# Layer 1 of a fused eight-stage kernel: attention and the mixture-of-experts routing written as one ordered loop

## The chip, the cores and the metric

The kernel runs on one core of a Trainium2 chip. The metric is device time in microseconds (us) of one execution. The comparison is against the kernel before, timed in the same way. A core has a matrix engine (PE in the profile, with its weight loads PEld), a vector engine (DVE), a scalar engine for activation functions (ACT), a general engine (POOL) that here also issues the indirect DMAs, and an engine that only issues DMAs (SP). Each engine works through its own queue of instructions in order; engines wait for each other by semaphores.

## The reference

The program is four layers, each an attention-like stage and a feed-forward stage, over 8192 tokens of width 128. The change touches layer 1 alone:

```python
# attention of layer 1 (T = 256 tokens in a sequence, 32 sequences)
xn = layer_norm(x, g, b)
q, k, v = split(xn @ qkv_w + qkv_b)
k = k * sigmoid(xn @ gate_w + gate_b)
q = elu(q) + 1.0
k = elu(k) + 1.0
attn = (q @ k.T) * tril
out = (attn @ v) / (sum(q * cumsum(k)) + 1e-6)
x = x + out

# feed-forward of layer 1: 8 experts of hidden width 512, two for each token, and one shared expert
xf = layer_norm(x)
logits = xf @ gate_w + gate_b
top_w, top_i = top_k(logits, 2)
gw = softmax(top_w)
for e in range(8):
    out += combine[:, e:e+1] * (gelu(xf @ w1[e] + b1[e]) @ w2[e] + b2[e])
x = x + out + gelu(xf @ ws1 + bs1) @ ws2 + bs2
```

Here elu(z) + 1 is max(z, 0) + exp(min(z, 0)).

## The kernel before

The 8192 tokens are 64 tiles of 128 tokens; four tiles make a block of 512 tokens (two sequences), so there are 16 blocks. The residual stream `K.x` stays in on-chip memory for the whole kernel. Instructions are ordered by a scheduler that works from priorities, except inside `manual_schedule`, where the engines named keep the order in which the program writes their instructions. POOL and SP are not named in the regions spoken of here, so their order is the scheduler's.

`l1_attn` (L1244 to L1336) has two halves. The first normalizes all tiles (`normed`, L134, on DVE), turns them on PE (`transpose4`, L141), scales them on ACT into `xnT` (L215), and then for each block computes the gated key `kg` (PE L1274 and L1275, ACT sigmoid L1277, DVE L1278). The second half, for each block, makes the query `qp` (PE L1288), the two elu functions (POOL minimum L1293, DVE minimum L1294, ACT exponentials L1295 and L1296, ACT relu L1297, DVE L1298, POOL addition L1299), the value `vp` with its bias as a one-row float32 matmul (PE L1301, L1305, ACT copy L1309), the products `at` (PE L1313, L1316), the mask (DVE L1321), the output `o` (PE L1325), and the division and residual (DVE L1330 to L1334). This half is not in an ordered region.

`l1_ffn` (L1340 to L1452) follows. It loads the weights of all nine experts, takes the statistics of all 64 tiles (L241 and the short chain in `Norm.steps`), normalizes and turns all tiles into `row` and `xnT`, and computes logits for all tokens with 8-column matmuls (PE L1389). Routing is then one chain on DVE for all 64 tiles: `beaten` ranks the eight logits, `picks` marks the two chosen experts, and `Slots.places` counts tokens per expert (two matmuls and a scan) and gives each token a slot in a DRAM table `rows` that is grouped by expert. `Slots.finish` works out which group of 256 slots belongs to which expert. Then each tile's rows are written to their slots by an indirect DMA, issued by POOL, twice for each tile since two experts are chosen:

```python
for n in range(2):
    S.belongs(row, 0, NT, n)
    nc.gpsimd.tensor_copy(row[:, :, D + 1], weight[:, n, :])
    for j in range(NT):
        S.send(slots[n][:, j : j + 1], row[:, j, :])
```

That is 128 calls of `send` (L473). `belongs` (L368) writes, on POOL, where the result of each row will go back. Beside the sends, the shared expert runs for 16 blocks (PE L1431 for the hidden layer, ACT gelu L1435, PE L1437 and L1443 for the output, DVE L1449 for the residual). Last, `Slots.experts` reads the table in 72 groups of 256 rows (SP fetch, PE, ACT, DVE) and scatters each group's result by two more indirect DMAs (POOL L479). It reads what any tile may have written, so its first fetch waits for the last send. Layer 2 starts after it.

Of the kernel before, what the change touches and what calls it, by code (L numbers as in the profile page):

```python
# [10 lines left out]
F32 = mybir.dt.float32  # L11
# [8 lines left out]
P = 128  # L20
# [1223 lines left out]
def l1_attn(K):  # L1244
    nc, ins = K.nc, K.ins
    with ExitStack() as es:
        sp = K.pool(es, "a1", 1)
        wk = K.pool(es, "a1w", 3)
        w = K.load(sp, "a1_w")
        wq, wkk, wv, wg = (w[:, i * D : (i + 1) * D] for i in range(4))  # L1250
        bv = K.load(sp, "a1_bv")
        cols = K.load(sp, "a1_cols")
        bq, bk, bg, gamma, beta = (cols[:, i : i + 1] for i in range(5))
        mean, r2 = K.norm_of_x.mean, K.norm_of_x.r2
        xnT = sp.tile([P, NBLK, 512], F32, name="xnT")
        kg = sp.tile([P, NBLK, 512], F32, name="kg")
# [6 lines left out]
        vs = [sp.tile([P, 4, D + 1], F32, name=f"v{i}") for i in range(2)]  # L1263
        for v in vs:
            nc.gpsimd.memset(v[:, :, D : D + 1], 1.0)

        with ExitStack() as ps:
            pp = K.pool(ps, "a1pt", 2, PSUM)
            pk = K.pool(ps, "a1pk", 2, PSUM)
            K.to_channels(xnT, pp, wk, (mean, r2), affine=(gamma, beta))  # L1270
            for blk in range(NBLK):
                gp = pk.tile([P, 512], F32, name="gp")
                kp = pk.tile([P, 512], F32, name="kp")
                nc.tensor.matmul(gp, wg, xnT[:, blk, :], start=True, stop=True)  # L1274
                nc.tensor.matmul(kp, wkk, xnT[:, blk, :], start=True, stop=True)  # L1275
                sg = wk.tile([P, 512], F32, name="sg")
                nc.scalar.activation(sg, gp, AF.Sigmoid, bias=bg)  # L1277
                nc.vector.scalar_tensor_tensor(kg[:, blk, :], kp, bk, sg, ALU.add, ALU.mult)  # L1278

        with ExitStack() as ps:  # L1280
            pq = K.pool(ps, "a1pq", 2, PSUM)
            pv = K.pool(ps, "a1pv", 2, PSUM)
            pa = K.pool(ps, "a1pa", 2, PSUM)
            po = K.pool(ps, "a1po", 2, PSUM)
            for blk in range(NBLK):
# [3 lines left out]
                q = wk.tile([P, 512], F32, name="q")  # L1289
                k = wk.tile([P, 512], F32, name="k")  # L1290
                qr = wk.tile([P, 512], F32, name="qr")
                kb = kg[:, blk, :]
                nc.gpsimd.tensor_scalar_min(k, kb, 0.0)  # L1293
                nc.vector.tensor_scalar(q, qp, bq, 0.0, ALU.add, ALU.min)  # L1294
                nc.scalar.activation(k, k, AF.Exp)  # L1295
                nc.scalar.activation(q, q, AF.Exp)  # L1296
                nc.scalar.activation(qr, qp, AF.Relu, bias=bq)  # L1297
                nc.vector.scalar_tensor_tensor(k, kb, 0.0, k, ALU.max, ALU.add)  # L1298
                nc.gpsimd.tensor_add(q, q, qr)  # L1299
                vp = pv.tile([P, 4, D], F32, name="vp")  # L1300
                nc.tensor.matmul(  # L1301
                    vp, K.ones, bv.unsqueeze(1).to_broadcast([1, 4, D]), start=True, stop=False
# [5 lines left out]
                v = vs[blk % 2]  # L1308
                nc.scalar.copy(v[:, :, 0:D], vp)  # L1309
                for b in range(2):  # L1310
                    c = b * SEQ
                    at = pa.tile([P, 3, P], F32, name="at")
                    nc.tensor.matmul(  # L1313
                        at[:, 0:2, :], k[:, c : c + P], q[:, c : c + SEQ], start=True, stop=True
                    )
                    nc.tensor.matmul(  # L1316
                        at[:, 2, :], k[:, c + P : c + SEQ], q[:, c + P : c + SEQ],
                        start=True, stop=True,
                    )
                    a = wk.tile([P, 3, P], F32, name="a")  # L1320
                    nc.vector.tensor_mul(a, at, mask)  # L1321
                    o = po.tile([P, 2, D + 1], F32, name="o")
                    for h, tiles in ((0, ((0, 0),)), (1, ((1, 0), (2, 1)))):
                        for n, (i, sh) in enumerate(tiles):
                            nc.tensor.matmul(  # L1325
                                o[:, h, :], a[:, i, :], v[:, 2 * b + sh, :],
                                start=n == 0, stop=n == len(tiles) - 1,
                            )
                    den = wk.tile([P, 2], F32, name="den")
                    nc.vector.tensor_scalar_add(den, o[:, :, D], 1e-6)  # L1330
                    nc.vector.reciprocal(den, den)
                    for h in range(2):
                        xj = K.x[:, 4 * blk + 2 * b + h, :]
                        nc.vector.scalar_tensor_tensor(  # L1334
                            xj, o[:, h, 0:D], den[:, h : h + 1], xj, ALU.mult, ALU.add
                        )  # L1336

def l1_ffn(K):  # L1340
    nc, ins = K.nc, K.ins
    NE, F = 8, 512
    FC = F // P
    S = K.slots1
    with ExitStack() as es:
        sp = K.pool(es, "f1", 1)
        gate_w = K.load(sp, "f1_gate_w")
        gate_b = K.load(sp, "f1_gate_b")

        LONG = 2 * F + FC + D  # L1350
        w_all = sp.tile([P, NE + 1, LONG], F32, name="w_all")
        for e in (NE, *range(NE)):
            nc.sync.dma_start(w_all[:, e, 0:F], ins["f1_w1"][e])
            nc.sync.dma_start(
                w_all[:, e, F : 2 * F].rearrange("p (c d) -> p c d", c=FC),
                ins["f1_w2"][e].rearrange("(c p) d -> p c d", p=P),
            )
        nc.sync.dma_start(
            w_all[:, :, 2 * F : 2 * F + FC], ins["f1_b1"].rearrange("p (e c) -> p e c", c=FC)
        )  # L1360
        mean, r = K.ln_stats(sp, K.x, "f1")
        expert = sp.tile([1, S.groups], mybir.dt.int32, name="expert")
        start = sp.tile([1, S.groups], mybir.dt.int32, name="start")
        S.begin(sp, NT)
        with ExitStack() as fs:
            fp = K.pool(fs, "f1a", 1)
            xnT = fp.tile([P, NBLK, 512], F32, name="xnT")
            row = fp.tile([P, NT, S.WIDE], F32, name="row")
            weight = fp.tile([P, 2, NT], F32, name="weight")
            cs = ExitStack()  # L1370
            cp = K.pool(cs, "f1c", 1)
            with ExitStack() as bs:
                K.second_biases(K.pool(bs, "f1b", 1), w_all[0:3, :, 2 * F + FC :], "f1_b2")
            pl = K.pool(cs, "f1pl", 1, PSUM)
            hw = K.pool(cs, "f1h", 2)
            ph = K.pool(cs, "f1ph", 3, PSUM)
            po = K.pool(cs, "f1po", 2, PSUM)
            for blk in range(NBLK):
                for j in range(4 * blk, 4 * blk + 4):
                    K.normed(row[:, j, 0:D], j, mean, r)  # L1380
                t = ph.tile([P, 512], F32, name="hp")
                K.transpose4(t, row[:, 4 * blk : 4 * blk + 4, 0:D])
                nc.scalar.copy(xnT[:, blk, :], t)
            lp = pl.tile([P, 2, NT * NE], F32, name="lp")[:, 0, :].rearrange("p (n e) -> p n e", e=NE)
            nc.tensor.matmul(
                lp, K.ones, gate_b.unsqueeze(1).to_broadcast([1, NT, NE]), start=True, stop=False
            )
            for j in range(NT):
                nc.tensor.matmul(  # L1389
                    lp[:, j, :], xnT[:, j // 4, j % 4 * P : (j % 4 + 1) * P], gate_w,  # L1390
                    start=False, stop=j == NT - 1,
                )
            lg = cp.tile([P, NT, NE], F32, name="lg")
            nc.scalar.copy(lg, lp)
            beaten = K.beaten(cp, lg)
            picks = [cp.tile([P, NT, NE], F32, name=f"pick{i}") for i in range(2)]
            top = cp.tile([P, NT, NE], F32, name="top")
            nc.vector.tensor_scalar(top, beaten, 1.5, None, ALU.is_lt)
            nc.vector.tensor_scalar(picks[0], beaten, 0.5, None, ALU.is_lt)
            nc.vector.tensor_sub(picks[1], top, picks[0])  # L1400

            m = cp.tile([P, NT], F32, name="m")
            nc.vector.tensor_reduce(m, lg, axis=AX.X, op=ALU.max)
            nc.vector.tensor_sub(lg, lg, m.unsqueeze(2).to_broadcast([P, NT, NE]))
            nc.scalar.activation(lg, lg, AF.Exp)
            nc.vector.tensor_mul(top, lg, top)
            nc.vector.tensor_reduce(m, top, axis=AX.X, op=ALU.add)
            nc.vector.reciprocal(m, m)
            for i in range(2):
# [1001 lines left out]
```

## Time and profile before

| what | value |
|---|---|
| time, median of 3 runs | 3505.45 us (3495.78 to 3506.91) |
| time of the profiled execution | 3373.54 us |
| span in the profiled execution, first to last instruction | 3371.8 us |
| mean granted PE clock in it | 0.89 |
| busy: PE, DVE, ACT, POOL | 2775.8, 1859.4, 1383.8, 866.2 us |
| layer 1 in the span, first weight load to first expert's transpose | 862.5 to 1283.0 us |

The stretch of layer 1 can be cut by the first and last instruction of its lines: the first half of attention from 862.5 to 915, the second half to 1017, statistics, normalization and logits to 1086, the routing chain to about 1115, the shared expert to 1207, and from there to 1283 only sends. "Busy" counts the time in which an engine has an instruction in work; "clock" is the share of its full speed that PE was granted, and matmuls at 0.5 take about twice as long. A row of the stage table gives the stretch, its length, the busy time and number of instructions of PE, PEld, DVE, ACT and POOL, the granted PE clock, the share of DMA engines in use, and GB/s.

### The profile page before, as it was taken

To read this page: it belongs to the slowest core of one execution; us is meant where nothing else is said; L and a number is where in the kernel's file an instruction comes from. 1 tells how busy PE (TensorE), PEld (TensorE's weight loads), DVE (VectorE), ACT (ScalarE), POOL (GpSimd) and SP (SyncE) were. 2 spreads that over 40 slices of the span, in tenths; PEclk is the share of its full clock that TensorE was granted. 3 is DMA by queue.
4 is the path that set the end of the run, shared out by engine and by line. 5 is a ranking of instruction groups with operands and counts; after the bars stand their busy time and mean duration, and the time that the engine had idled before them with its cause. 6 is when DMAs were issued, how large, how long until landed. Compare 5 with 4: busy or idle time off the path is not lost. (4 is left out here: it accounts for less than half of the span.)

```text
span 3371.8 us, 59245 instructions
## 1 busy us (share of the span) xinstructions
PE 2775.8 (82%) x21882; PEld 1895.8 (56%) x21884; DVE 1859.4 (55%) x4791; ACT 1383.8 (41%) x2892; POOL 866.2 (26%) x1230
## 2 busy tenths in 40 slices
PE   5999778999997927999588999978778888888490
PEld 4765444447576616888366666657444455555370
DVE  6115445436665303333567666655668877775447
ACT  3323432223632302333345555541425566666123
POOL 0001344300130674444100000000113412233463
PEclk9899789999996968999589999986868999999695
DMA  2377465510001111222544444400033343432233
GB/s 66 118 251 222 180 239 226 222 61 3 4 1 57 41 51 55 61 61 59 159 122 135 128 128 123 118 22 1 7 101 103 102 124 113 133 115 60 73 92 106
DMA packets 262840, 340.80 MB, mean 101 GB/s; under 512 B 34182, under 2 KB 230642, under 8 KB 254360
## 3 DMA queue, kind: packets, MB, share of 16 engines
q1 hardware_dynamic: 230808, 237.00, 24.5%
q0 software_dynamic: 27584, 97.92, 7.7%
q8 instruction: 174, 2.85, 0.4%
q10 hardware_dynamic: 4160, 2.10, 0.2%
q14 instruction: 114, 0.93, 0.1%
HBM read 156.71 MB, written 177.83 MB: 99 GB/s over the span
## 5 line engine op out<-in xcount | busy, mean ns | idle before, releaser
L1636 DVE TENSOR_REDUCE top<-s 128x6 f32<-128x768 f32 (+1 forms) x512 | 556.9, 1088 | 204.6 <-PE s L1549 71.3
L1686 ACT ACTIVATE e<-t 128x384 f32<-128x384 f32 (+1 forms) x1024 | 508.8, 545 | 205.0 <-PE t L1549 111.1
L1678 PE MATMUL t<-q,k 64*128 64x256 f32 (+1 forms) x2048 | 426.5, 311 | 23.3 <-ACT e L1686 21.6
L1623 PE MATMUL s<-k,q 48*128 48x256 f32 (+1 forms) x2048 | 428.1, 335 | 8.7 <-DVE top L1636 8.5
L1678 PEld LDWEIGHTS t<-q,k 64*128 64x128 f32 x2048 | 301.4, 195 | 130.8 <-ACT e L1686 57.9
L1698 PE MATMUL o<-e,val 128*32 128x256 f32 (+1 forms) x4096 | 311.4, 377 | 0.0
L1623 PEld LDWEIGHTS s<-k,q 48*128 48x128 f32 x2048 | 301.6, 202 | 16.7 <-DVE top L1636 13.2
L539 ACT ACTIVATE h<-hp,w 128x256 f32<-128x256 f32 x368 | 154.3, 470 | 377.9 <-PE hp L533 376.2
L479 POOL DMA_INDIRECT f_back<-y,place x224 | 215.7, 963 | 241.5 <-DVE y L555 183.5
L549 PE MATMUL o<-w,h 128*128 128x128 f32 x1472 | 213.7, 284 | 0.0
L533 PE MATMUL hp<-xT,w 128*128 128x256 f32 x736 | 195.1, 405 | 9.7 <-DVE xT L524 9.7
L549 PEld LDWEIGHTS o<-w,h 128*128 128x128 f32 x1472 | 182.8, 192 | 7.8
L1850 POOL TENSOR_SCALAR xn<-x_sb,mean_x,r_x 128x128 f32<-128x128 f32 x64 | 52.3, 825 | 488.6 <-PE m L1572 448.1
L533 PEld LDWEIGHTS hp<-xT,w 128*128 128x128 f32 x736 | 134.3, 195 | 33.2 <-DVE xT L524 12.0
L1549 PE MATMUL s<-hideq,pick 64*128 64x128 bf16 x1024 | 148.1, 233 | 0.0
L1549 PE MATMUL t<-hidek,pick 64*128 64x128 bf16 x1024 | 147.3, 227 | 0.0
L515 DVE COPY w<-w_all 128x1028 f32 (+1 forms) x112 | 67.7, 604 | 135.1 <-POOL mk L1516 84.1
L555 DVE TENSOR_TENSOR y<-o,xs 128x256 f32<-128x256 f32 x112 | 47.5, 424 | 162.2 <-PE o L553 162.1
L473 POOL DMA_INDIRECT f_rows<-row,slot x128 | 123.0, 961 | 43.3 <-issue 38.4
L766 PE MATMUL up<-wc,hT 128*128 128x128 f32 x768 | 129.1, 309 | 0.0
L141 PE MATMUL t<-ident,xn 128*128 128x128 f32 x320 | 72.2, 352 | 66.7 <-DVE xn L134 50.2
L522 PE MATMUL t<-ident,xs 128*128 128x128 f32 x224 | 44.6, 282 | 99.1 <-DMA xs<-f_rows 99.1
(507 smaller groups left out, 5546.9 us busy)
## 6 DMA issues: line engine op xcount, KB each, us to landing
f_rows<-blank POOLq DMA_DIRECT2D x176, 390.0 KB, 2.7
d<-half SPq DMA_DIRECT2D x256, 256.0 KB
tz<-kpad SPq DMA_DIRECT2D x64, 512.0 KB
q<-d SPq DMA_DIRECT2D x128, 256.0 KB
k<-d SPq DMA_DIRECT2D x128, 256.0 KB
xs<-f_rows SPq DMA_DIRECT2D x112, 130.0 KB
t<-f_back SPq DMA_DIRECT2D x24, 512.0 KB
y_d<-ys SPq DMA_DIRECT2D x32, 256.0 KB
```

Of the source, the lines that this page charges most:

```text
L473: i = self.K.nc.gpsimd.indirect_dma_start(self.rows, bass.IndirectOffsetOnAxis(ap=slot, axis=0), row, None)
L479: i = self.K.nc.gpsimd.indirect_dma_start(self.back, bass.IndirectOffsetOnAxis(ap=place, axis=0), row, None)
L533: nc.tensor.matmul(hp[:, i, :], w[:, (c + i) * P : (c + i + 1) * P], xT, start=True, stop=True,)
L539: nc.scalar.activation(h[:, c + i, :], hp[:, i, :], act, bias=w[:, b1 : b1 + 1])
L549: nc.tensor.matmul(o[:, i, :], h[:, c, i * P : (i + 1) * P], w[:, F + c * D : F + c * D + D], start=c == 0, stop=False,)
L766: nc.tensor.matmul(o, hT[:, 2 * blk + b, s : s + P], wc[:, j, cs], start=j == 0, stop=False)
L1549: nc.tensor.matmul(t.rearrange("p (n q) -> p n q", n=3)[:, 0:3:2, 64 * n : 64 * n + 64], pick[r, n, :], hide[name][r], start=False, stop=n ...
L1623: nc.tensor.matmul(s[:, j, lo:hi], q[r, p, h * P : (h + 1) * P], k[r, p, 0 : hi - lo], start=h == 0, stop=not causal and h == 1,)
L1636: nc.vector.tensor_reduce(tops[b][:, :, :, p].rearrange("q h j -> q j h"), out_of["s"][:, :, 0:used].rearrange("q j (h k) -> q j h k", h=n ...
L1678: nc.tensor.matmul(t[:, kh * SEQ : kh * SEQ + SEQ - late], k[r, p, kh * P : (kh + 1) * P], q[r, p, late:SEQ], start=kh == 0, stop=not caus ...
L1686: nc.scalar.activation(e, t, AF.Exp)
L1698: nc.tensor.matmul(o[32 * i : 32 * i + 32, late:SEQ], val[b % RING][:, kh, 4 * g + i, :], exps[4 * g + i][:, kh * SEQ : kh * SEQ + SEQ - l ...
```

## The change

`l1_attn` and `l1_ffn` become one function, `layer1`. The first half of attention is as before. Its second half becomes an ordered loop (PE, ACT and DVE) of 18 steps over the 16 blocks: step n does `third(n-2)` (output, division, residual, and the statistics of these four tiles), `second(n-1)` (the products and the mask), `first(n)` (query, value, elu), and then `beside`, which advances the routing of tiles that are finished. Both minima of elu go: ACT computes relu(-z) and then exp(-relu(-z)). The bias of the value becomes a three-row bfloat16 matmul.

Routing goes in chunks of 16 tiles. `settle` does the normalization constants (20 short DVE instructions) and the 16 normalized tiles (now on ACT); `gate`, once a step, turns one block and computes the logits of the block before it; `choose` finds the two experts by maxima instead of `beaten`, takes the slots, and issues the chunk's 32 sends. `settle` and `choose` are generators; each round of `beside` runs each active one to its next `yield`, 10 rounds to a step of the attention loop and 14 to a step of the shared expert's loop, which is ordered too (`rise(n)`, `fall(n-1)`, `beside`). The shared expert's weights are loaded at the start, the other experts' after attention, and the second biases are prepared at the start. `row`, `xnT` and the rest of the stage's memory now stay allocated until the experts are done.

```diff
+        def settle(lo):
+            hi = lo + CHUNK
+            for _ in after.steps(lo, hi):
+                yield
+            nc.vector.scalar_tensor_tensor(
+                nmr[:, lo:hi], after.mean[:, lo:hi], -1.0, after.r[:, lo:hi], ALU.mult, ALU.mult
+            )
+            yield
+            for j in range(lo, hi):
+                nc.scalar.activation(
+                    row[:, j, 0:D], K.x[:, j, :], AF.Identity, bias=nmr[:, j : j + 1],
+                    scale=after.r[:, j : j + 1],
+                )
+                if j % 4 == 3:
+                    ready.append(j // 4)
+                yield
...
+        def gate(pt, pl):
+            count = [g for g in active if hold.get(g[1])][:1]
+            new = ready.pop(0) if ready else None
+            old = turned.pop() if turned else None
+            if new is not None:
+                t = pt.tile([P, 512], F32, name="t")
+                K.transpose4(t, row[:, 4 * new : 4 * new + 4, 0:D])
...
+            if old is not None:
+                out = u[:, 0 : 4 * NE].rearrange("p (n e) -> p n e", n=4)
+                for i in range(4):
+                    nc.tensor.matmul(
+                        out[:, i, :], xnT[:, old, i * P : (i + 1) * P], gate_w, start=True,
+                        stop=True,
+                    )
+            if new is not None:
+                nc.scalar.copy(xnT[:, new, :], t)
+                turned.append(new)
...
+            yield from S.places(rw, lambda: hold.pop(lo), picks, slots)
...
+            for i in range(2):
+                S.belongs(row, lo, n, i)
+                if i == 1:
+                    nc.gpsimd.tensor_copy(w0, weight[:, lo:hi])
+                for j in range(lo, hi):
+                    S.send(slots[i][:, j - lo : j - lo + 1], row[:, j, :])
+            yield
...
+        def beside(pt, pl, n):
+            gate(pt, pl)
+            for _ in range(n):
+                for g in list(active):
+                    go(g)
...
-                nc.gpsimd.tensor_scalar_min(k, kb, 0.0)
-                nc.vector.tensor_scalar(q, qp, bq, 0.0, ALU.add, ALU.min)
-                nc.scalar.activation(k, k, AF.Exp)
-                nc.scalar.activation(q, q, AF.Exp)
-                nc.scalar.activation(qr, qp, AF.Relu, bias=bq)
+                nc.scalar.activation(km, kb, AF.Relu, scale=-1.0)
+                nc.scalar.activation(k, km, AF.Exp, scale=-1.0)
+                nc.scalar.activation(qm, qp, AF.Relu, bias=nbq, scale=-1.0)
+                nc.scalar.activation(qr, qp, AF.Relu, bias=bq)
+                nc.scalar.activation(q, qm, AF.Exp, scale=-1.0)
...
+                after.take(K.x, 4 * blk, 4 * blk + 4)
+                if (4 * blk + 4) % CHUNK == 0:
+                    active.append((settle(4 * blk + 4 - CHUNK), None))
+            with K.tc.manual_schedule(
+                engines={nc.tensor.engine, nc.scalar.engine, nc.vector.engine}
+            ):
+                for n in range(NBLK + 2):
+                    if n >= 2:
+                        third(n - 2)
+                    if 1 <= n <= NBLK:
+                        second(n - 1)
+                    if n < NBLK:
+                        first(n)
+                        _, k, _, kb = held[n]
+                        nc.vector.scalar_tensor_tensor(k, kb, 0.0, k, ALU.max, ALU.add)
+                    beside(pt, pl, 10)
...
+                for n in range(NBLK + 1):
+                    if n < NBLK:
+                        rise(n)
+                    if n:
+                        fall(n - 1)
+                    beside(pt, pl, 14)
+                nc.scalar.copy(w_all[0:3, :, 2 * F + FC :], b2[:, 0:NE, :])
+                S.finish(rw, LONG, expert, start)
```

## The prediction

> **What bounds the kernel now.** I read first the table of stages, cut at the first and last instructions of layer 1's lines:
>
> ```profile
> 780.00:856.00 76.00, 71.20 (x583) 67.15 (x582) 60.99 (x133) 34.17 (x118) 0.00 (x0) 0.98 0.00 1
> ...
> 960.00:1012.00 52.00, 48.70 (x267) 35.27 (x266) 33.03 (x100) 18.74 (x33) 19.45 (x15) 1.00 0.00 1
> ...
> 1019.00:1086.00 67.00, 51.46 (x203) 40.76 (x204) 32.84 (x144) 12.75 (x21) 0.00 (x0) 0.52 0.25 71
> 1086.00:1118.00 32.00, 31.53 (x174) 21.64 (x175) 30.03 (x66) 15.15 (x21) 5.22 (x5) 1.00 0.01 4
> 1118.00:1207.00 89.00, 85.62 (x477) 58.83 (x476) 9.77 (x19) 30.12 (x44) 66.18 (x71) 1.00 0.16 52
> 1207.00:1283.00 76.00, 0.04 (x1) 0.07 (x2) 1.17 (x3) 0.00 (x0) 57.00 (x65) 0.50 0.16 53
> ```
>
> Attention (960) is close to PE-bound; normalization and logits (1019) run at half clock with no engine full; and in the last row PE does nothing for 76 us while POOL issues sends. Next, POOL's timeline, for the pace of the sends, and what frees the experts:
>
> ```profile
> 1275.44 0.95 POOL L473 DMA_INDIRECT f_rows<-row,slot  x1 [0.30 <-issue]
> 1276.70 0.96 POOL L473 DMA_INDIRECT f_rows<-row,slot  x1 [0.30 <-issue]
> 1277.97 0.96 POOL L473 DMA_INDIRECT f_rows<-row,slot  x1 [0.31 <-issue]
> ...
> 1282.96 0.66 PE L522 MATMUL t<-ident,xs 128*128 128x128 f32 x2 [79.34 <-DMA xs<-f_rows]
> ```
>
> A send takes 1.263 us start to start, whatever else runs: 128 take 162 us. They start at 1114.7, end at 1278.9, and the experts' first transpose comes 4 us later. So layer 1 is a chain: attention to 1017, routing for all tiles to 1115, sends to 1279. The shared expert, done at 1207, is off it.
>
> PE's timelines give the prices of the work that is moved:
>
> ```profile
> 984.19 1.02 PE L1288 MATMUL qp<-xnT,w_a_w 128*128 128x512 f32 x2
> 985.05 1.50 PE L1325 MATMUL o<-v,a 128*128 128x129 f32 x12
> 986.48 1.12 PE L1301 MATMUL vp<-w_a_bv,ones_row 1*128 1x512 f32 x2
> 987.53 1.16 PE L1305 MATMUL vp<-w_a_w,xnT 128*128 128x128 f32 x8
> 989.15 0.70 PE L1313 MATMUL at<-q,k 128*128 128x256 f32 x2 [0.46 <-POOL q L1299]
> ...
> 1084.91 0.96 PE L1389 MATMUL lp<-w_f_gate_w,xnT 128*128 128x8 f32 x8
> 1085.73 1.10 PE L1431 MATMUL hp<-xnT,w_all 128*128 128x512 f32 x2
> ...
> 1124.26 0.38 PE L1437 MATMUL o<-b,every 3*128 3x512 bf16 x1
> 1124.57 3.84 PE L1443 MATMUL o<-w_all,h 128*128 128x128 f32 x32
> ...
> 1131.78 0.38 PE L1437 MATMUL o<-b,every 3*128 3x512 bf16 x1
> ```
>
> Start to start: an attention block 6.37 us (0.46 of it a wait), its value bias 1.05, a three-row bfloat16 bias 0.31, a block's eight logit matmuls 0.82 at full clock, a shared-expert block 7.52.
>
> **The change, part by part.** What decides is when the first chunk's sends can start, and whether POOL is fed from then on. Both can be counted in the code. `settle` has 36 yields (19 statistics, one nmr, 16 rows), `choose` reaches its sends at its 26th round. Chunk 0's `settle` enters at step 5; its rows fall in steps 7 and 8; blocks 0 to 3 are turned in steps 8 to 11, the last logits come in step 12; `choose` runs in steps 12, 13, 14, and its sends go out in step 15. The same count puts chunk 1 in step 0 of the shared expert's loop, chunk 2 in step 3, chunk 3 in step 7. A chunk costs POOL 32 x 1.263 = 40.4, 0.5 for two `belongs` and a copy, and 2.0 before the second `belongs`, which overwrites a column that the first 16 sends read (the row of L368 shows that wait, 2.0): 43 us. Chunks 1 to 3 are there about 23, 46 and 76 us after chunk 0, POOL wants them at 43, 86 and 129. So from chunk 0 on POOL never starves: 172 us to the last send.
>
> When is step 15? The first half starts at 862.5 and PE needs 39 us for 64 transposes and 64 matmuls of 0.43 from 866; today the second half's exponentials mix in and ACT reloads its table (7 loads of 1.28 us for L1277 alone), so it lasts to 915. Unmixed I take 906. The second biases' split is seven DVE operations, 8.3 us by its rows at 625 (L101 to L107); then it hid between two stages, now it can land where DVE normalizes the first tiles: between 0 and 9, I take 3, since PE's later work absorbs part. So the loop starts at 909.
>
> A step without routing: PE 6.37 - 0.46 - 0.74 (cheaper bias) = 5.2. DVE loses the minimum (0.75), gains four statistics (4 x 0.24): 4.3. ACT gains two relu, 3.9; relu, copy and exponential share a table (no reload after 923), and the rows' identity shares it too in layer 3. But the order closes a chain: qp (0.96 with its latency), three ACT operations (2.1), POOL's addition (1.4), the next products (1.5) before the next qp: 6.0. That is the step. POOL's minimum (1.48) leaves a queue that was not full: nothing. With routing, PE adds four transposes (0.53) and eight logit matmuls (0.82): 6.4. `settle` puts 20 DVE operations of 0.18 in two steps (layer 3 has the same ones: 0.17 to 0.19), `choose` 30 operations, 0.17 to 0.4 (between layer 3's rows of 64 elements, 0.22, and here of 512, 0.7): 7.6 us a chunk, so a step of `choose` plus `settle` makes DVE 7 to 9.8. The 16 rows on ACT at 0.48 (L2279) fall ten in one step and six in the next: 4.8 us ahead of the next query's relu in ACT's queue, behind which POOL's addition and PE's products wait. Summed: step 0 3.5; 1 to 4 24; 5 and 6 12.6; 7 and 8 17; 9 and 10 13; 11 and 12 18; 13 and 14 16.8; to POOL's addition in step 15 4.5: 109 us. Chunk 0 starts at 1018, POOL ends at 1190, the first expert's transpose is at 1194 instead of 1283: 89.
>
> The shared expert: the loop ends about 1038, then 16 x 7.52 + 2 for filling, and six blocks turned, seven given logits: 9 more, 1169. It is covered by 21 us of sends; without them it would be the bound. `finish` (about 5 us of DVE, L435 to L464) comes after it, under the same cover. The exponentials of chunks 2 and 3 force four table loads, 5.1 us, on an ACT that is busy 2.75 of 7.52. SP's 24 expert loads go from 1018 to 1038; they took 13 us to issue and the experts need them at 1190. SP's loads at the start go behind the query's weights, which are first used 4 us after they land. POOL's constants (1.6 us at 1017) move to the start, where POOL idled 22 us. The stage's memory is held longer: layer 2's masks on POOL (2.2 us at 1280) move behind the experts, where POOL idled 15 us: 0, or 2 if all shows; I take 1 off, and get 88 to 89, say 90 with rounding of a sum this loose.
>
> **Two rules against it.** The table gives 780 to 856 a clock of 0.98 with four transposes among sixteen matmuls per 2.2 us. The Trainium skill (TensorE: Matmul & The Clock Gate, Part 4: PE-mode transpose) says that transposes do not count as busy for the clock. That fits 1019 to 1086 (0.52, transposes and 8-column matmuls alone). By the rule, pushed onto the loop, steps 8 to 17 run at half clock: ten steps of 6.4 more, a saving of 26. By the row, mixed transposes cost nothing; I take the row.
>
> Sends now run beside a busy DVE. The Trainium skill (SBUF — State Buffer, the "DVE blocks DMA" trap under the engine-port model) says that a vector copy in a two-port mode keeps POOL from writing descriptors: 620 ns become 3100. This trace has such a pair in the experts:
>
> ```profile
> 1398.16 0.96 POOL L479 DMA_INDIRECT f_back<-y,place  x1 [2.22 <-DVE y L555]
> 1398.30 0.70 DVE L515 COPY w<-w_all 128x1028 f32 x1 [0.42 <-DVE y L555]
> ```
>
> The copy lies inside the DMA's issue, which still took its 0.96. By the rule, some 20 copies and scalar operations of 0.18 (in `settle` of chunk 3 and `choose` of chunks 1 to 3) hold one send each, for 0.2 us or, at the page's ratio, 2.5: 4 to 50 us less saved. By the row, nothing; I take nothing, and the slower rival below holds the rest.
>
> **The sum against the times.** 3373.5 - 90 = 3283.5 in the profiled execution. The three timed runs lie 132 us (3.9%) above it, and the page cannot say where. The gain is one of POOL's pace and of order, so I carry 90 us over unscaled (94 if scaled): 3415.
>
> **Rivals.**
> Loop slower: in-order waits that I cannot see make the steps 9 us instead of 7; chunk 0 leaves 40 us later, gain 50, 3455. For it: three engines near 7 us a step and single buffers for qp and vp. Against: before's block at half clock, waits included, took 8.7.
> Loop faster: early rows and full queues let PE set the pace, 5.2 to 6.4; chunk 0 leaves at 988, gain 120, 3385; the shared expert would then end at 1139 and not bind.
> The change does not do what it says: if the scheduler takes `row` as one piece, ACT's later rows wait for all sends of earlier chunks, two stalls of 42 us; end near 1251, gain 32, 3473. Against: `K.x`, as large, is written by tile today without such a wait.
> Slower: the half clock holds wherever routing rides along and spreads to its neighbours. Place: the loop and steps 0 to 6 of the shared expert. PE's 87 us up to step 15 become 174, the loop ends near 1100, seven blocks of 8.8 take 123, nine 68: 1293, then `finish`: 1298, 15 later, 3520. It decides from the point where PE's end passes 1283, 114 us beyond mine. The row of 780 speaks against it.
>
> **How the numbers follow.** Forecast 0.59, faster loop 0.13, slower loop 0.18, `row` as one piece 0.03, half clock 0.07 (0.04 slower, 0.03 near zero, where only part of it holds). About 0.3% is what a measurement of this kernel tells from no change. Faster 0.93, same 0.03, slower 0.04. The range takes the forecast (70 to 110), the slower loop to 40 and the faster to 137 (with the scaling, and no loss to the biases): 3368 to 3465.
>
> **What would show it.** Right: 128 sends at 1.26 us, in four groups of 32 with gaps of 2 to 3 us, the first about 155 us after the stage's weights load; clock near 1.0 in the loop; PE idle 20 to 30 us before the experts instead of 76. Wrong: POOL idle between groups; a first send later than 1040; clock 0.5 in the loop; PE still at the shared expert when the last send leaves.

## The result and the profile after

The changed kernel takes 3460.76 us (median of 4 runs, 3451.04 to 3463.56), the kernel before 3506.18 beside it (3495.78 to 3515.17): a ratio of 0.9867, 95% interval 0.9833 to 0.99. The gain is 45 us, half of the 90 forecast. The runs fell on several chips, and the kernel before takes 3490 to 3519 us on one of them (A below) and 3356 to 3390 on three others (B), so the comparison above is by its times one of A, while the profile of 3373.54 us that the prediction was worked out on has the time of B.

The stage table of the changed kernel, cut at the sends (columns: stretch, its length, busy time and number of instructions of PE, PEld, DVE, ACT and POOL, granted PE clock, DMA share, GB/s):

```profile
909.00:960.00 51.00, 45.58 (x206) 29.56 (x205) 27.36 (x86) 27.52 (x45) 7.62 (x6) 0.93 0.00 0
960.00:1020.00 60.00, 55.60 (x360) 43.79 (x358) 52.67 (x199) 46.31 (x95) 11.54 (x9) 1.00 0.01 1
1020.00:1080.00 60.00, 30.16 (x154) 21.73 (x153) 18.86 (x94) 21.33 (x40) 42.12 (x45) 0.78 0.39 116
1080.00:1115.00 35.00, 4.22 (x5) 1.15 (x4) 0.08 (x1) 0.02 (x1) 21.46 (x24) 0.50 0.13 44
1115.00:1150.00 35.00, 24.07 (x113) 15.91 (x114) 9.54 (x33) 16.61 (x30) 0.00 (x0) 0.76 0.00 0
1150.00:1192.00 42.00, 20.54 (x103) 13.78 (x102) 1.77 (x5) 4.03 (x7) 30.24 (x34) 0.77 0.15 48
1192.00:1221.00 29.00, 22.67 (x104) 15.06 (x105) 8.55 (x30) 10.60 (x15) 0.81 (x1) 0.81 0.02 5
1221.00:1264.00 43.00, 22.89 (x113) 14.96 (x112) 1.38 (x2) 5.28 (x8) 31.06 (x34) 0.81 0.15 48
1264.00:1310.00 46.00, 41.18 (x232) 29.02 (x232) 5.28 (x9) 14.45 (x21) 0.00 (x0) 0.92 0.01 2
```

Up to 1020 the stretch ends as forecast: the loop runs at a clock of 0.93 to 1.00 and the first send leaves at 1020.56. Then the table alternates. Where POOL is busy (1080, 1150, 1221) DVE and ACT do little or nothing, and PE works 4.2 us of 35 in the first of these stretches and about half of the two others; where POOL has no sends (1115, 1192, 1264) all three work. POOL's timeline shows what it waited for at the third and the fourth chunk, and PE's timeline when the first expert begins:

```profile
1150.56 0.96 POOL L473 DMA_INDIRECT f_rows<-row,slot  x1 [40.78 <-ACT h L1558]
...
1221.26 0.96 POOL L473 DMA_INDIRECT f_rows<-row,slot  x1 [28.45 <-ACT h L1558]
```
```profile
1320.31 0.66 PE L522 MATMUL t<-ident,xs 128*128 128x128 f32 x2 [11.53 <-DMA xs<-f_rows]
```

POOL starved for 69.2 us in two places. The releaser named, the gelu of the shared expert, is only the last thing that happened in a loop whose DVE part chooses the slots. The routing of chunks 2 and 3 came late because the loop had stopped: `a_last` below has the same order without the stops, and there it is not late. How it stopped shows in PE's timeline beside chunk 1's sends, and in what DVE and ACT do at the end of it (of the view of all engines, DVE and ACT):

```profile
1069.28 0.62 PE L1338 MATMUL u<-w_f_gate_w,xnT 128*128 128x8 f32 x5
1070.77 0.17 PE L1338 MATMUL u<-w_f_gate_w,xnT 128*128 128x8 f32 x1 [0.87 <-issue]
1072.17 0.17 PE L1338 MATMUL u<-w_f_gate_w,xnT 128*128 128x8 f32 x1 [1.23 <-issue]
1074.27 0.17 PE L1338 MATMUL u<-w_f_gate_w,xnT 128*128 128x8 f32 x1 [1.93 <-issue]
1076.37 1.01 PE L1554 MATMUL hp<-xnT,shared 128*128 128x512 f32 x1 [1.93 <-issue]
1079.16 1.01 PE L1554 MATMUL hp<-xnT,shared 128*128 128x512 f32 x1 [1.78 <-issue]
...
1120.81 2.07 PE L1554 MATMUL hp<-xnT,shared 128*128 128x512 f32 x2 [30.13 <-ACT h L1558]
```
```profile
1108.83 0.96 POOL L473 DMA_INDIRECT f_rows<-row,slot  x1 [0.30 <-issue]
1114.92 0.69 DVE L1574 TENSOR_TENSOR x_sb<-x_sb,o 128x512 f32<-128x512 f32 x1 [57.40 <-remote]
1114.98 0.59 ACT L1343 COPY xnT<-t 128x512 f32<-128x512 f32 x1 [50.92 <-remote]
```

PE waits for nothing that the profile knows ("issue"), yet its instructions start 1.40, 2.10 or 2.80 us apart, multiples of 0.70. The matmuls that ACT's copy and DVE's addition wait for ended by 1069.4 (transposes) and 1069.0 (shared expert's output). Both start at 1114.9, 45 us later, and 6 us after the issue of the last of the 48 sends that make up chunk 0's second group and chunk 1. The trace's record of the semaphore that PE counts up says the same: the six matmuls that count it and end from 1069.0 to 1090.7 are all counted between 1114.90 and 1115.18. So while POOL issues a long row of sends, PE issues slowly and its completions reach nobody until the row is over; the sends themselves go on at 1.26 us each. A pause of 2.4 us within the row (1087.5 to 1089.8, where POOL waits for its sends to land) freed nothing.

### The profile page after: what moved, and what is told of

Read it like the earlier page. It is cut to its first block, busy times and chain, and to the rows that moved or that the text cites. A ratio compares the mean times of both kernels' runs of the same rounds, so it can differ in the third digit from the quotient of the medians.

```text
span 3457.9 us, 59352 instructions
## 1 busy us (share of the span) xinstructions
PE 2776.9 (80%) x21871; PEld 1889.7 (55%) x21872; DVE 1848.1 (53%) x4833; ACT 1417.3 (41%) x2985; POOL 840.9 (24%) x1225
## 5 line engine op out<-in xcount | busy, mean ns | idle before, releaser
L1554 PE MATMUL hp<-xnT,shared 128*128 128x512 f32 x128 | 73.4, 703 | 107.8 <-ACT h L1558 77.8
L473 POOL DMA_INDIRECT f_rows<-row,slot x128 | 123.2, 963 | 112.9 <-ACT h L1558 69.2
L1574 DVE TENSOR_TENSOR x_sb<-x_sb,o 128x512 f32<-128x512 f32 x16 | 11.0, 688 | 209.9 <-remote 99.0
```

The lines of the kernel that those rows point to most:

```text
L473: i = self.K.nc.gpsimd.indirect_dma_start(self.rows, bass.IndirectOffsetOnAxis(ap=slot, axis=0), row, None)
```

## Experiments

**Before once more, and the change where before is quick.** Kernel `b_again` is before, unchanged.

> The kernel before once more, unchanged, to find where its usual 3505 us differ from the 3373.5 of the execution that the prediction was worked out on. Theory A (while POOL issues a run of indirect sends, PE's completions reach the other engines late, and what waits for PE stands still): the 130 us lie where sends run beside PE's work, some 60 to 120 in the shared expert beside the 128 sends (its blocks take well over 7.52 us, PE is still at it when the last send leaves) and 40 to 60 in layer 3's attention (a pair of batches with 8 sends takes over 25 us instead of 19). Theory B (a lower clock, or slower memory, all over): every stage is about 4% longer and the shared expert's blocks still take about 7.5 to 7.8 us.

It took 3366.38 us: a chip of kind B, so the extra 130 us could not be looked for there. It repeats the first profile (layer 1's weights at 858.2, first expert's transpose at 1278.4: 420 us). Its stage table beside the sends is the picture that the prediction had taken for the rule, PE busy without a break for 89 us while POOL sends:

```profile
1110.00:1199.00 89.00, 89.00 (x489) 60.50 (x488) 13.43 (x27) 32.20 (x47) 66.05 (x71) 1.00 0.16 51
1199.00:1276.00 77.00, 0.31 (x3) 0.11 (x2) 0.00 (x0) 0.00 (x0) 57.42 (x60) 0.53 0.16 53
```

Kernel `a_last` was meant to hold the sends back until the shared expert's loop is over:

```diff
             yield
+            later.append((lo, hi, w0, slots))
+            yield
+
+        def leave(lo, hi, w0, slots):
             for i in range(2):
-                S.belongs(row, lo, n, i)
+                S.belongs(row, lo, hi - lo, i)
...
                 S.finish(rw, LONG, expert, start)
+                for chunk in later:
+                    leave(*chunk)
```

> The changed kernel with all 128 sends of layer 1 kept back until the shared expert's loop and the planning of the experts are over; everything else stands where it was. Theory A (sends hold up the loop): without sends beside it the shared expert runs at its 7.5 us a block, the loop and its routing end at 1165 to 1180 instead of 1309, no stretch of over 4 us leaves PE, ScalarE and VectorE idle together, and the 162 us of sends come after that: the first expert near 1340, the time 3460 to 3475. Theory C (the loop's own order, its single buffers and waits make the routing of chunks 2 and 3 late, whatever POOL does): the loop still ends near 1300, the sends end near 1462, the time is about 3590 to 3620.

The edit missed its aim: POOL's queue is not in the order written by hand, and the scheduler put the sends back where they had been. Every engine has the same instructions in the same order as in the changed kernel, so this is a repetition of the change, on B. It took 3278.59 us, with before at 3390.32 on the same chip and 3366.38 as `b_again` there: a gain of 88 to 112. These are single executions. Its stage table, POOL's last send and PE's timeline:

```profile
960.00:1015.00 55.00, 51.16 (x334) 40.59 (x332) 47.91 (x184) 42.84 (x89) 10.24 (x8) 1.00 0.00 1
...
1042.00:1118.00 76.00, 64.94 (x347) 46.20 (x347) 15.96 (x52) 30.29 (x50) 56.22 (x61) 0.89 0.21 67
1118.00:1166.00 48.00, 48.00 (x261) 32.28 (x260) 8.23 (x21) 17.43 (x26) 35.26 (x39) 1.00 0.16 52
1166.00:1190.00 24.00, 17.11 (x111) 12.94 (x109) 6.43 (x13) 5.48 (x8) 17.06 (x20) 0.96 0.14 47
```
```profile
1189.66 1.37 POOL L473 DMA_INDIRECT f_rows<-row,slot  x1 [0.30 <-issue]
```
```profile
1194.91 0.66 PE L522 MATMUL t<-ident,xs 128*128 128x128 f32 x2 [11.79 <-DMA xs<-f_rows]
```

The first send left at 1015.6, the last at 1189.7, the first expert began at 1194.9, beside the forecast's 1018, 1190 and 1194. Same instructions, same order, same pace of sends as in the changed kernel on A; only the standing still is missing.

Kernel `a_last_plain` adds to `a_last`, at the sends' places, 128 plain transfers of the same tiles from SP (`self.spare[n * P : n * P + P] <- row[:, j, 0:D]`).

> The kernel with the sends kept back, and at their former places 128 plain transfers of the same 64 KB tiles from SyncE's queue into memory that nothing reads: the bytes without POOL's issuing. If the transfers themselves (their packets on the DMA engines) hold up the loop, it ends near 1300 again and the time is 3590 to 3620. If it is POOL's issuing, or the shape of the indirect transfers, the loop ends at 1165 to 1185 and the time lies within 15 us of the kernel with the sends kept back.

3278.32 us. As the sends had not moved and the chip was of kind B, this tells only that 128 further transfers of 64 KB cost nothing beside the loop there.

**The changed kernel again, on A.** Kernel `a_again` is the changed kernel itself.

> The changed kernel once more. The kernel with the sends kept back turned out to have the same order on POOL as the changed one (its first send left at 1015.6, its last at 1189.7), so it was a repetition of it, in executions in which before took 3366 to 3390. Theory A, in the form that is left (the stand-still beside sends belongs to the condition in which an execution finds the chip, and strikes both kernels): where before takes 3366 to 3390 in this run, the changed kernel takes 3275 to 3290, all sends in one stretch from 1016 to 1190, the gain 90 to 110; where before takes about 3505, the changed one takes 3450 to 3465 with POOL idle between the groups. Theory C (the first run's idle POOL is the loop's own, and the kept-back sends had removed it by their other buffers): 3310 to 3345 even where before takes 3380.

Before took 3498.78 us, the changed kernel 3445.17; ratio 0.9847 (0.982 to 0.9873), a gain of 54. That is theory A's second case (forecast 3450 to 3465, five below its edge). Again POOL waited 62.2 us at chunks 2 and 3, and the stretches of layer 1 over 4 us long with PE, ACT and DVE all idle sum to 64.5 us, all of them beside sends or up to 5 us after the last one. Theory C, that the loop's own order makes the routing late, falls: with the same order nothing is late on B.

**What before does on A, and the elu alone.** Kernel `b_elu` is before with two relu and two exponentials on ScalarE in place of the two minima.

```diff
-                nc.gpsimd.tensor_scalar_min(k, kb, 0.0)
-                nc.vector.tensor_scalar(q, qp, bq, 0.0, ALU.add, ALU.min)
-                nc.scalar.activation(k, k, AF.Exp)
-                nc.scalar.activation(q, q, AF.Exp)
...
+                nc.scalar.activation(km, kb, AF.Relu, scale=-1.0)
+                nc.scalar.activation(k, km, AF.Exp, scale=-1.0)
+                nc.scalar.activation(qm, qp, AF.Relu, bias=nbq, scale=-1.0)
                 nc.scalar.activation(qr, qp, AF.Relu, bias=bq)
+                nc.scalar.activation(q, qm, AF.Exp, scale=-1.0)
```

> The kernel before with the change's elu alone: two relu and two exponentials on ScalarE in place of a minimum on VectorE and one on POOL. The prediction put POOL's minimum at nothing, because PE set the pace of a block (6.37 us). Right if the time is within 5 us of before and the blocks of attention take 6.2 to 6.5 us. If POOL's minimum was in the chain that a block waits for, 8 to 15 us faster; if ScalarE's two further operations (0.96 us a block) delay the copy of the values, up to 10 us slower.

3487.59 against 3498.78: 11 us faster, ratio 0.9958 (0.994 to 0.9976), so the forecast "within 5" was wrong and the minima were in the way (which of the two, this run does not tell). PE's start-to-start time of a block of attention is 6.03 us (`qp` at 936.42 and 942.46) instead of 6.37, and PE has no wait left for POOL's addition, for which before waited 4.2 us in nine blocks. From the first query to the last it takes 105.1 us instead of 115.8 in `b_again`. Of these 10.7 us, 4.4 are gained in the last ten blocks; the rest lies earlier, where both halves of attention overlap (one gap between two queries is 23.4 us instead of 30.1).

More important is what this kernel, which differs from before in attention alone, shows of before on A (stage table):

```profile
1098.00:1118.00 20.00, 18.58 (x87) 12.15 (x85) 6.83 (x17) 4.68 (x7) 14.97 (x16) 0.91 0.15 47
1118.00:1183.00 65.00, 5.21 (x10) 2.10 (x9) 0.69 (x1) 2.10 (x4) 48.20 (x52) 0.52 0.15 51
...
1204.00:1274.00 70.00, 0.25 (x1) 0.00 (x0) 0.69 (x1) 0.00 (x0) 44.37 (x47) 0.50 0.13 45
1274.00:1342.00 68.00, 64.44 (x330) 43.44 (x330) 5.50 (x8) 23.94 (x35) 0.00 (x0) 0.92 0.00 1
```

The first 16 sends leave PE alone, then it stops; half of the shared expert (68 us) is done after the last send. From the first weights to the first expert's transpose it takes 485 us (861.0 to 1346.1), and before would take some 496 with the 11 that the elu saves (an estimate): 76 more than on B. The other part of the 130 us lies in layers that the change does not touch: in layer 3, which has 64 sends beside its attention, it is 829 us from the weights to the first expert's transpose instead of 789, and from there to the end 212 instead of 199.

**Sends away from the loop.** Kernel `a_late` is `a_last` with one DVE write after the planning, to the column of places, which each chunk's first POOL operation must wait for:

```diff
                 S.finish(rw, LONG, expert, start)
+                nc.vector.memset(row[:, :, D], 0.0)
                 for chunk in later:
```

> The changed kernel with the sends really held: a DVE write to the column of places after the planning, which every chunk's first POOL operation must wait for. The loop then runs with no send beside it. If sends beside the loop cost it nothing, it ends at 1165 to 1172 as with them (the prediction: 1169), 128 sends and their groups' waits take 170 more, the first expert's transpose is near 1340, the time 140 to 150 us above the changed kernel in the same condition. If the sends slow the loop by x us even in a quick execution, it ends x earlier than there, and the time is 150 - x above. In the slow condition (before 3505) the loop still ends at 1165 to 1180 instead of 1309 and the time is 3485 to 3495.

On A: 3508.45 us, where 3485 to 3495 was expected. Stage table:

```profile
1040.00:1118.00 78.00, 64.01 (x330) 45.42 (x331) 15.93 (x52) 33.56 (x55) 0.00 (x0) 0.88 0.09 26
1118.00:1194.00 76.00, 67.64 (x386) 47.73 (x384) 15.62 (x40) 22.91 (x33) 0.34 (x4) 0.95 0.00 1
1194.00:1362.00 168.00, 0.00 (x0) 0.00 (x0) 0.00 (x0) 0.00 (x0) 124.16 (x137) 0.50 0.16 52
```

No stretch with all three engines idle is left in the loop, on the chip where the changed kernel has 64.5 us of them; the shared expert ends at 1186.4 instead of 1309 or 1299. So it is the sends beside it. From the end of the stage before (865.5) that is 320.9 us; in `a_last` on B, with all the sends beside it, it is 321.2 (862.6 to 1183.8): there they cost the loop nothing that shows. The time missed its range because loop and planning ended at 1193.6, where I had put 1165 to 1180.

Kernel `a_late_plain` adds the plain transfers from SP to `a_late`, which would tell the bytes from POOL's issuing.

> All sends held until the loop is over (3508 in the condition where before takes 3499), and 128 plain transfers of the same 64 KB tiles by SyncE's queue at the former places, into memory that nothing reads. If the bytes on the DMA engines are what holds up PE's completions, the loop stops as with sends: it ends at 1280 to 1310 instead of 1194, and the time is 3590 to 3620. If it is POOL's issuing of indirect sends (or their many small packets), the loop ends at 1190 to 1205 and the time is within 15 us of 3508. Where before takes about 3380 neither would show, and the time is about 3430.

3432.79 us with before at 3377.03: a chip of kind B, where neither could show (forecast there about 3430). Whether plain transfers would hold PE up on A stays open, and with it whether it is the bytes or POOL's issuing.

**Shorter rows of sends.** Kernel `a_chunk8` has `CHUNK = 8` and 16 and 20 rounds of routing a step.

> Chunks of 8 tiles instead of 16, with 16 and 20 rounds of routing a step instead of 10 and 14. If the first send and POOL's pace set the end, as the prediction had it: the first send leaves some 30 us earlier (about 985), the eight groups take 128 x 1.263 + 8 x 2.5 = 182 us and end at 1167 to 1172, and the shared expert's loop, which ended at 1165 to 1170, becomes the bound: 10 to 20 us below the changed kernel. If DVE is the loop's bound (twice as many routing operations for the same tiles, some 150 of 0.18 us more), the first send leaves only after 1000 and the shared expert ends 10 to 20 us later than before: no gain, or a loss of up to 15.

On A: 3398.7 us, ratio 0.9723 (0.969 to 0.9757), 46 less than the changed kernel beside it. More than an earlier start could give: the first send left at 979.4 (38 earlier), but the first expert began at 1260.9 instead of 1309.9. The rows of sends were 8 long with about 2 us between them, where POOL waits for its sends to land before it writes the column of places again, and one stop of over 4 us was left (5.2 us, at 1113, at the end of a row of 16). Start and row length were both changed here, so the next kernels change the rows alone.

Kernel `a_pause8` keeps chunks of 16 and writes the places once more in the middle of each group:

```diff
                     S.send(slots[i][:, j - lo : j - lo + 1], row[:, j, :])
+                    if j - lo == 7:
+                        S.belongs(row, lo, n, i)
```

> The changed kernel, chunks of 16, with the column of places written again after the first eight sends of each group: the same values, so that nothing changes but that POOL must wait there until its eight sends have landed (about 2 us, eight times). Theory A1 (what stands still beside sends does so only after a long unbroken row of them: groups of 8 with 2 us between them, as with chunks of 8, leave PE's completions time to get through): where before takes about 3500, the stretches with PE, ScalarE and VectorE all idle shrink from 92 us to under 40, POOL no longer starves by 70 us, and the time is 3365 to 3410 instead of 3445; where before takes about 3380, the pauses only cost: 3278 + 17, about 3295. Theory A2 (every send costs the loop about the same, and chunks of 8 gained only by their earlier start): where before takes about 3500, 3440 to 3465.

On B: 3293.4 us, ratio 0.976 (0.9711 to 0.9809), the price of the pauses as forecast (3295).

> The kernel with a pause after the first eight sends of each group once more, because its first run was in the condition in which before takes 3377, where it could only show the price of the pauses (3293, forecast 3295). Theory A1 (the stand-still needs a long unbroken row of sends): where before takes about 3500, the stretches with PE, VectorE and ScalarE all idle shrink from 92 us to under 40 and the time is 3365 to 3410, against 3445 to 3461 of the changed kernel. Theory A2 (every send costs the loop the same): 3440 to 3465. Where before takes about 3380 again: 3285 to 3305, and the question stays open.

B again: 3301.55, ratio 0.9809 (0.9763 to 0.9855). Kernel `a_pause8_r14` is `a_pause8` with `beside(pt, pl, 14)` in the attention loop.

> The kernel with the pauses after eight sends, and in the attention loop 14 rounds of routing a step instead of 10. Counted from the yields, settle then takes three steps instead of four and choose two instead of three, so chunk 0's sends leave one or two steps (6 to 13 us) earlier; the size is small against what the pauses should tell. Where before takes about 3500: theory A1 (the stand-still needs a long unbroken row of sends) 3355 to 3405, with the idle stretches under 40 us; theory A2 (every send costs the loop the same) 3430 to 3460. Where before takes about 3375: 3283 to 3293 if the first send leaves near 1006, and 3293 to 3305, nothing gained, if VectorE's longer rounds stretch the steps by what they save.

On A: 3398.72 us, ratio 0.9693 (0.9656 to 0.973), 46 to 62 less than the changed kernel. Theory A1's range was 3355 to 3405, A2's 3430 to 3460. Stage table:

```profile
1010.00:1049.00 39.00, 21.52 (x120) 16.83 (x119) 21.52 (x90) 17.12 (x36) 28.20 (x31) 0.81 0.13 42
1049.00:1110.00 61.00, 39.40 (x172) 28.82 (x173) 16.26 (x68) 20.59 (x37) 31.27 (x36) 0.73 0.34 102
1110.00:1170.00 60.00, 38.76 (x175) 25.18 (x175) 9.79 (x34) 14.30 (x21) 40.30 (x46) 0.78 0.14 46
1170.00:1226.00 56.00, 54.55 (x296) 36.45 (x296) 8.19 (x21) 18.58 (x28) 31.71 (x37) 0.99 0.12 40
```

PE now works beside the sends in every stretch. The idle stretches of over 4 us sum to 16.5 us in layer 1, against 64.5. The longer of the two left, 1049.4 to 1059.4, has another cause: PE waits for an addition that stands behind a row of eight sends in POOL's own queue.

```profile
1059.37 1.22 PE L1491 MATMUL at<-q,k 128*128 128x256 f32 x2 [16.92 <-POOL q L1482]
```

The first expert began at 1258.9, 51 us earlier. The first send left 6.5 us earlier (1010.5), and I put no more than that down to the 14 rounds; no run has them alone on A. That pauses in the rows keep the loop from stopping fits this run and `a_chunk8`; both changed the start as well.

Kernel `a8_l3pause2` is `a_chunk8` with a wait after every second send of layer 3.

> Chunks of 8 in layer 1, and in layer 3, whose 64 sends go out eight at a time beside its attention, the column of places written again after every second send, so that POOL waits for them to land. Theory A1 (long unbroken rows of sends): where before takes about 3500, layer 3's attention, 683 us there against 640 to 647 in the quick executions, comes down to 645 to 660, and the time is 25 to 40 below the 3399 of the chunks of 8 alone: 3360 to 3375. Theory A2 (each send costs its own 1 us or so, in whatever grouping): layer 3 keeps its 683, the time 3390 to 3405. Where before takes about 3380 there is nothing to gain: 3265 to 3280.

On B: 3346.64, ratio 0.9919 (0.9887 to 0.9951), 67 above the range that I had set there. Layer 3 takes 807 us from its weights to its first expert (796 in `a_last`), so its pauses cost 11 us at most; chunks of 8 are the main cause. The first expert begins at 1241.1 instead of 1194.9, for the shared expert ends only at 1230.3 although the sends are done at 1171. So chunks of 8, on A as good as the pauses, lose 46 of the 85 us that layer 1 gains on B. What slows PE in that loop I did not take apart. Whether pauses help layer 3 on A stays open.

## Why the prediction came out as it did

The time fell inside the range by luck: the range went down to a gain of 40 for steps of 9 us in the loop, and that is not what took half of the gain. The steps of the sum, in order:

- **When the first send leaves** (forecast 1018): 1015.6, 1017.0 and 1020.6 in the three profiles. The count of yields was right, but the sum came out by two errors that cancel. In `a_last` the loop begins at 917.0, not 909, and from its first query to the first send it takes 98.6 us, not 109: steps are 5.7 us without routing, where 6.0 was forecast, and 6.3 to 7.8 with it, where the sum had up to 9. The late start is mostly the splitting of the biases, put at 3 us. It takes 10.5 us of DVE, and all of it comes ahead of the first normalized tile, which is 12 us later than in the profile of before (second fence):

```profile
867.69 0.75 DVE L101 CAST hi_f_b<-rows 3x1152 bf16<-3x1152 f32 x1
...
878.03 0.18 DVE L1290 COPY bv<-rows_bv 3x128 bf16<-3x128 bf16 x1
878.25 0.86 DVE L134 TENSOR_SCALAR xn<-x_sb,mean_x,r_x 128x128 f32<-128x128 f32 x3
```
```profile
866.21 0.35 DVE L134 TENSOR_SCALAR xn<-x_sb,mean_x,r_x 128x128 f32<-128x128 f32 x1 [0.47 <-issue]
```

- **POOL never starves, 172 us to the last send**: on B no wait for routing, and 174 us; on A 62 to 69 us of starving, and 235 to 242 us. This is the step that failed. It rested on another that the prediction did not cost at all, that sends run "whatever else runs" and that the rest runs whatever is sent. The first half of that holds on both kinds of chip (1.26 us each); the second does not on A.
- **The shared expert's end, 1169, covered by 21 us of sends**: 1183 on B, covered by 6, since PE waits 16.6 us for ACT's gelu while the routing's rows go past it, and the clock is 0.89 there. On A it ends at 1309, after the last send.
- **The first expert at 1194 instead of 1283**: on B 1194.9. First weights to first expert are 335 us (from 860.1) instead of 420, a gain of 85. On A they are 448 in `a_again` (861.6 to 1309.9) instead of about 496, a gain of 48.
- **"I carry 90 us over unscaled"**: here the half was lost. The difference of 132 us between profile and times was named and passed over; it was the sign that something beside the sends costs more where the times were taken. There before loses 76 us in layer 1 and the changed kernel 114. It loses more because its routing lies beside the sends: when the loop stops, the next chunk's slots are late and POOL, which never had to wait before, starves.
- **POOL's minimum at nothing**: `b_elu` gained 11 us from both minima. The sum was not hurt, because its new step had been counted from the chain and not from the old block.
- **Half clock in the loop**: the row was right. The clock was 1.00 in 960 to 1020, with the routing's transposes mixed in; by the rule of the Trainium skill (TensorE: Matmul & The Clock Gate, Part 4: PE-mode transpose), pushed onto this loop, 64 us of the gain would have gone and 26 been left.
- **Vector copies holding sends**: with the routing's copies beside the sends, the issue of a send has a median of 0.96 to 0.97 us in every run and a maximum of 1.45. (The 2.5 us of the prediction is the difference of the page's two figures, not their ratio.) The 3.1 us that the Trainium skill gives for its trap (SBUF — State Buffer, "DVE blocks DMA") appear nowhere. What happened was the reverse of it: POOL was not held up; the engines beside it were.

Two of the signs that the prediction had named for "wrong" did appear on A: POOL idle between groups, and PE still at the shared expert when the last send leaves.

## What to carry to other kernels

Work that lies beside a run of indirect DMAs is not free until an execution under the timed conditions shows it so; where the profiled execution is 4% quicker than the timed ones, look for what the difference is before a gain is carried over. If a producer of a queue's work runs beside that queue, a stop of the producer can be paid twice, once for its own work and once in the queue's starving: on A before loses 76 us in this layer and the changed kernel 114. Sends in rows of eight with a wait for landing between them cost 15 to 23 us where nothing stands still (beside single executions without the waits) and gained 46 to 62, with slightly earlier sends, where it does. And work that is moved to the start of a stage may stand ahead of all of it: the biases' splitting hid between two stages before and costs 10.5 us at the head of the new one.

## What was not expected of the hardware

The same program with the same instruction order took 3278 us on one chip and 3445 on another; the slow chip, met again by `a_pause8_r14`, had before at 3503 us there too. On A the standing still begins after a row of about 8 to 16 sends and mostly ends 3 to 6 us after the last one. In `b_elu` single completions came through while the sends went on, 5.5 to 6.3 us apart (ACT's gelus start at 1165.53, 1171.06, 1176.66 and 1182.96). PE issues on a beat of 0.70 us meanwhile, and SP too (its loads at 1039.79, 1040.50 and 1041.20 in the changed kernel), while the sends keep 1.26 us and their packets are no slower (mean 101 ns in 1044 to 1084 on A and on B). PE fetches 16 KB of instructions at a time, and it issued as many between two fetches across the standing still (242) as elsewhere (240 to 257). Which path it is that PE's issue and completions share with POOL's sends on that chip, and why only there, the runs do not settle.
